# Layer 1 on rows X with W applied behind its loop, attention scalars from raw rows in the last chunk, and a different way to rank the last tile

## The chip, the cores and the metric

The kernel runs on one core of one Trainium2 chip. The core has five engines with their own instruction streams: TensorE (PE in the profile, its weight loads PEld), VectorE (DVE), ScalarE (ACT), GpSimd (POOL) and SyncE (SP, which only issues DMAs here). They meet through semaphores. The metric is the device time of one launch in microseconds; a time below is the median of several executions.

## The reference

There are N = 2708 nodes with D = 128 features, and a dense 2708 x 2708 array `adj` with positive entries where there is an edge. Four layers follow each other, each ending in `x = layernorm(x + layer(x))`.

```python
# layer 0: graph Laplacian with 4 nearest neighbours added
z = leaky_relu(lap(adj, x) @ W1 + b1, 0.1)
S = exp(-sqrt(dist2(z, z) + 1e-10) / 2)        # keep the 4 best of each row
out0 = lap(topk(S) + adj, x) @ W2 + b2         # lap(A, x) = d * (A @ (d * x)), d = rowsum(A) ** -0.5
# layer 1: attention
XW = X @ W
r, c = XW @ a[128:], XW @ a[:128]              # one number a node each
den = exp(leaky_relu(r[:, None] + c[None, :], 0.01))
num = adj @ den
H = adj @ (where(num != 0, den / num, 0) @ XW)
# layers 2 and 3: normalized adjacency, then a linear map; plain adjacency, concat, linear, relu
```

Layer 1 is the costly one: `den` is a full 2708 x 2708 array. Its entry depends only on r of the row, c of the column and the sign of r + c, so for columns sorted by c each row has one cut. The kernel sorts the nodes by c, works on blocks of the sorted order, and forms `adj @ (att @ XW)`. Since `att @ (X @ W)` equals `(att @ X) @ W`, W may stand on either side of that loop.

## The kernel before

Nodes are cut into T = 22 tiles of 128 rows, t = 0 to 21; the last one, t = 21 (`T - 1`, also called `FULL`), has only `LAST` = 20 rows. Columns of `adj` are cut into C = 6 chunks of 512, 512, 512, 512, 384 and 276, which are the tiles 0-3, 4-7, 8-11, 12-15, 16-18 and 19-21. Of the transposed adjacency, the row tiles from 16 on stay in SBUF (`res`); the other 16 are read again in each pass as panels of four tiles (`load_panel`, L178, on SP's queue) into a ring of four slots.

The stages, with their place in the profiled execution:

- Pass 1 of layer 0 and its z (to about 163 us), then the search for the nearest neighbours (to about 305 us): products of z (L647), then DVE's MAX8 and FIND_INDEX8 a tile. Near its end the rows `y2` (scaled input rows) are made and written to DRAM as `y2_rows` by `weigh` (L614, L618). The last write, with tiles 20 and 21, stands on SP's queue; the first panel load of chunk 1 is put behind it with `issue_after`.
- Pass 2 (about 295 to 430 us), `by_panels` with the products at L204. It takes chunk after chunk, 22 products each. After every product `Due.tick` runs the small steps that have come due; `end_pass2` gives each step its tick, counted from the tick n at which its chunk ends. So the code of a step fixes its place in TensorE's, DVE's and ACT's order, which is kept as written (`manual_schedule`). SP and POOL place their own instructions by a scheduler.
- In pass 2, `sum_near` gathers the neighbours' rows of `y2_rows` by indirect DMA on POOL (L677, three a tile) and DVE adds them up (L690); TensorE adds the sum to its accumulator (L697). Then for each chunk: ACT copies the accumulator to hT (L837); `norm0` multiplies by W2 (L725), adds the residual (L730) and normalizes (L276 to L281); `turn` transposes xs (L742) and copies it to xT (L744); `find_c` multiplies xT by the vector `w_c` (L749), which gives c in every row, copies it into `c_row` (L750, the same memory as hT) and takes each row's own c from the diagonal (L754); `times_w` multiplies xT by W, with the two attention vectors as columns 129 and 130 (L762), and copies to `xwe` (L763); `keep_xw` writes the rows to DRAM (L768, POOL).
- The rank of a node by c is counted in the same pass. `compare` makes for tile t a mask of c_row >= c for the columns up to its own (L784, 128 rows; L779 for the last tile, 20 rows by 2708 columns with DVE's own row sum). `rank_rows` sums it along the row on ACT (L797), `rank_columns` sums it down each earlier column block on TensorE (L802, one column of PSUM an earlier tile). `own_ties` (L786) settles equal values in the tile itself.
- After chunk 5, the last one, all this stands alone: its products are done. DVE forms the ranks `rk_f` (L924 to L928), picks out the c at chosen ranks (`pick_c`, L937 to L942, first a coarse `head`, then `first`), TensorE spreads one to all rows (L948), DVE makes `lc` (L977 to L982), finds each node's block (L991 to L1010), and the one-hot arrays (L1018, L1035, L1039). TensorE transposes r onto all rows (L913, `on_all`). Then it begins the block sums (`part_sum`, L1181, about 451 to 508 us), into which `between` puts the rest of the sorting.
- Layer 1's block loop (about 508 to 733 us): for each block of sorted nodes, a gather of adjacency rows (L1306), num (L1428), the reciprocal (L1260 to L1277), and the sum of `att @ XW` with gathered rows of `xw_rows` (L1285, accumulators hacc).
- The result mT is copied (L160 on ACT, L162 on DVE), transposed back to rows by tile (the first ten at L1496, inside the loop; twelve at L1513), scaled (L1498, L1514) and multiplied by `adj`, then layers 2 and 3 by L204 (about 735 to 1066 us).

Of the kernel before, what the change touches and what calls it, by code (L numbers as in the profile page):

```python
# [52 lines left out]
def kernel(  # L53
# [135 lines left out]
    def by_panels(weights, done, tick=None, ready=(), first=None, behind=None):  # L189
# [16 lines left out]
        for c in range(C):  # L206
            w = cw[c]
            for i in [*(first if first and c == 0 else range(FULL)), *([FULL] if c % GROUPS == 0 else [])]:
# [7 lines left out]
                if i < S:  # L216
                    if i % 4 == 0:
                        if ready:
                            part = ready.pop(0)
                        elif behind is not None:  # L220
                            with tc.issue_after(behind):
                                part = load_panel(i // 4, c)
                            behind = None
                        else:
                            part = load_panel(i // 4, c)
                    src = part[:, i % 4, :w]
                else:
                    src = res[:, i - S, cols[c]]
# [138 lines left out]
    xw_rows = dram.tile([N, D], F32, tag="xw_rows", name="xw_rows")  # L367
    with tc.tile_pool(name="knn", bufs=1) as knn:
# [178 lines left out]
        wae = atile([D + 2], "wae")  # L547
        nc.vector.tensor_copy(wae[:, :D], wa_sb)
        for n, half in enumerate((1, 0)):
# [3 lines left out]
                op0=ALU.mult, op1=ALU.mult, accum_out=wae[:, D + n : D + n + 1],  # L553
            )
        w_c = atile([P], "w_c")
        nc.vector.tensor_copy(w_c, wae[:, D + 1 :].to_broadcast([P, P]))
# [33 lines left out]
        def weigh(ts):  # L590
# [22 lines left out]
            queue = nc.gpsimd if t1 < T else nc.sync  # L613
            ins = queue.dma_start(  # L614
                y2_rows[t0 * P : full * P, :].rearrange("(t p) d -> p t d", p=P), y2[:, t0:full, :]
            )
            if full < t1:
                ins = queue.dma_start(y2_rows[FULL * P :, :], y2[:LAST, FULL, :])  # L618
# [3 lines left out]
            return ins.ins  # L622
# [3 lines left out]
        with tc.tile_pool(name="keys", bufs=3) as keys:  # L626
# [28 lines left out]
            written = weigh(range(T - 2, T))  # L655
# [10 lines left out]
    wide = ctx.enter_context(tc.tile_pool(name="wide", bufs=1))  # L666
    xwe = wide.tile([P, T, D + 1], F32, tag="wide", name="xwe")
# [42 lines left out]
    if LAST:  # L710
        nc.gpsimd.memset(xwe[:, FULL, :], 0.0)
        nc.gpsimd.memset(cc[:, FULL:], 0.0)
# [4 lines left out]
    rows_d = atile([T], "rows_d")  # L717
    nc.vector.memset(rows_d, 0.0)
# [3 lines left out]
    def norm0(ts, power=False):  # L722
# [11 lines left out]
        normalize(ts, xs, power)  # L734
# [3 lines left out]
    def turn(c):  # L738
        pt = mis_tile()
        for t in chunk_tiles[c]:  # L740
            o = t * P - starts[c]
            nc.tensor.transpose(pt[:, o : o + pw[t]], xs[: pw[t], t, :], ident[: pw[t], : pw[t]])  # L742
        xTs[c] = sum_pool.tile([P, CW], F32, tag="xT", name="xT", bufs=3)
        nc.scalar.copy(xTs[c][:, : cw[c]], pt[:, : cw[c]])  # L744

    def find_c(c):

        pc = mis_tile()
        nc.tensor.matmul(pc[:, : cw[c]], lhsT=w_c, rhs=xTs[c][:, : cw[c]], start=True, stop=True)  # L749
        nc.scalar.copy(c_row[:, cols[c]], pc[:, : cw[c]])  # L750
        for t in chunk_tiles[c]:
            p, o = pw[t], t * P - starts[c]
            own = small.tile([P, P], F32, tag="junk", name="own")
            nc.vector.scalar_tensor_tensor(  # L754
                own[:p, :p], pc[:p, o : o + p], 1.0, ident[:p, :p], op0=ALU.mult, op1=ALU.mult,
                accum_out=cc[:p, t : t + 1],
            )

    def times_w(c, t):
        p, o = pw[t], t * P - starts[c]  # L760
        po = mis_tile()
        nc.tensor.matmul(po[:p, : D + 1], lhsT=xTs[c][:, o : o + p], rhs=wae[:, : D + 1], start=True, stop=True)  # L762
        nc.scalar.copy(xwe[:p, t, : D + 1], po[:p, : D + 1])  # L763

    def keep_xw(c):
        ts = chunk_tiles[c]
        t0, t1 = ts[0], min(ts[-1] + 1, FULL)
        nc.gpsimd.dma_start(  # L768
            xw_rows[t0 * P : t1 * P, :].rearrange("(t p) d -> p t d", p=P), xwe[:, t0:t1, :D]
        )  # L770
        if t1 <= ts[-1]:
            nc.gpsimd.dma_start(xw_rows[FULL * P :, :], xwe[:LAST, FULL, :D])

    def compare(t):
        p, o = pw[t], t * P
        s = cc[:p, t : t + 1]
        mask = masks[t] = sum_pool.tile([P, N], BF16, tag="mask", name="mask", bufs=3)
        if t in by_dve:
            nc.vector.tensor_scalar(  # L779
                mask[:p, : o + p], c_row[:p, : o + p], s, 0.0, op0=ALU.is_ge, op1=ALU.add,  # L780
                accum_out=rows_m[:p, t : t + 1],
            )
        else:
            nc.vector.tensor_scalar(mask[:p, : o + p], c_row[:p, : o + p], s, None, op0=ALU.is_ge)  # L784
        eq = small.tile([P, P], F32, tag="junk", name="eq")
        nc.vector.scalar_tensor_tensor(  # L786
            eq[:p, :p], c_row[:p, o : o + p], s, not_before[:p, :p], op0=ALU.is_equal, op1=ALU.mult,
# [3 lines left out]
    by_dve = (T - 1,)  # L791

    def rank_rows(t):
        p, w = pw[t], t * P + pw[t]
        if t not in by_dve:
            junk = sum_pool.tile([P, N], BF16, tag="copy", name="junk")
            nc.scalar.activation(junk[:p, :w], masks[t][:p, :w], AF.Copy, accum_out=rows_m[:p, t : t + 1])  # L797

    def rank_columns(t):
        p = pw[t]  # L800
        for u in range(t):
            nc.tensor.matmul(  # L802
                rk[:, u : u + 1], lhsT=masks[t][:p, u * P : (u + 1) * P], rhs=ones_b[:p, :1],
                start=(t == 1 and u == 0), stop=(t == T - 1), skip_group_check=True,
            )


# [5 lines left out]
    def find_r():  # L813
        nc.vector.tensor_copy(rr, xwe[:, :, D])
# [15 lines left out]
    def end_pass2(c, acc):  # L830
# [9 lines left out]
        if c < C - 1:  # L840
            at(n + 2, norm0, ts)
            at(n + 9, turn, c)
            at(n + 11, find_c, c)
            for k, t in enumerate(ts):
                at(n + 13 + 2 * k, compare, t)
                at(n + 14 + 2 * k, times_w, c, t)
                if k == len(ts) - 1:
                    at(n + 14 + 2 * k, keep_xw, c)
                if c == C - 2 and k == len(ts) - 1:
                    behind_last.append(t)  # L850
                else:
                    at(n + 16 + 2 * k, rank_rows, t)
                if t:
                    at(n + 17 + 2 * k, rank_columns, t)
        else:
            for t in behind_last:
                at(n + 1, rank_rows, t)
            at(n + 1, exp_table)
# [765 lines left out]
```

## Time and profile before

| what | value |
|---|---|
| time, median of 3 | 1070.3 us (1069.45 to 1070.99) |
| the profiled execution | 1068.2 us, span 1066.5 us |
| mean granted TensorE clock | 0.976 |
| PE busy | 990.4 us, 93% of the span |
| DVE busy | 643.2 us, 60% |
| ACT busy | 339.1 us, 32% |
| POOL busy | 265.6 us, 25% |
| moved by DMA | 190.30 MB, mean 178 GB/s |

The page of a profile gives busy time, then the span in 40 equal slices, then the chain of work that ended last, then groups of instructions. A line "L204 PE ..." is an instruction written at line 204 of the kernel before. A wait "PE acc L697 <- DVE near_sum L690" says that TensorE stood still before an instruction of L697 until one of L690 had ended on DVE. In the chain each line is a start, a length and the work that the end of the program hangs on.

### The profile page before, as it was taken

To read this page: it belongs to the slowest core of one execution; us is meant where nothing else is said; L and a number is where in the kernel's file an instruction comes from. 1 tells how busy PE (TensorE), PEld (TensorE's weight loads), DVE (VectorE), ACT (ScalarE), POOL (GpSimd) and SP (SyncE) were. 2 spreads that over 40 slices of the span, in tenths; PEclk is the share of its full clock that TensorE was granted. 3 is DMA by queue.
4 is the path that set the end of the run, shared out by engine and by line. 5 is a ranking of instruction groups with operands and counts; after the bars stand their busy time and mean duration, and the time that the engine had idled before them with its cause. 6 is when DMAs were issued, how large, how long until landed. Compare 5 with 4: busy or idle time off the path is not lost.

```text
span 1066.5 us, 11423 instructions
## 1 busy us (share of the span) xinstructions
PE 990.4 (93%) x3678; PEld 479.8 (45%) x3678; DVE 643.2 (60%) x1351; ACT 339.1 (32%) x614; POOL 265.6 (25%) x332
## 2 busy tenths in 40 slices
PE   0898999999998999699899999999999999999996
PEld 0345554444434566444333333334444544564444
DVE  5985438999954678764789999995121111132222
ACT  0000125555510235603767777663010100010000
POOL 4000000000447664107774444440121100000000
PEclk9989999999999999699999999999999999999998
DMA  9999350000056756399655546456765856575652
GB/s 338 367 342 249 115 166 1 0 1 1 22 199 211 239 175 207 126 341 306 165 160 131 147 135 164 137 151 208 226 198 173 291 196 202 159 256 170 225 173 67
DMA packets 109363, 190.30 MB, mean 178 GB/s; under 512 B 13650, under 2 KB 46690, under 8 KB 109294
## 3 DMA queue, kind: packets, MB, share of 16 engines
q1 hardware_dynamic: 91582, 151.86, 43.8%
q0 software_dynamic: 17712, 37.62, 12.7%
q8 instruction: 31, 0.51, 0.2%
q14 instruction: 38, 0.31, 0.1%
HBM read 214.37 MB, written 4.16 MB: 205 GB/s over the span
## 4 chain that ended last, share of the span: by engine, by line
PE 80%; DMA 7%; DVE 6%; issue 2%; POOL 2%; ACT 2%; SPq 1%; POOLq 0%; DVEq 0%; ACTq 0%
PE acc L204 34%; PE acc L647 9%; PE hacc L1285 9%; PE num L1428 9%; PE acc L432 7%; DMA res<-in_adjT 3%; PE acc L637 3%; PE acc L1181 2%; DMA got<-y_rows,where 1%; PE mis L289 1%; DMA part<-in_adjT 1%; DVE mask L784 1%; DVE both L487 1%; POOL ring L125 1%; PE mis L1192 1%
## 5 line engine op out<-in xcount | busy, mean ns | idle before, releaser
L1306 POOL DMA_INDIRECT ring<-in_adjT,slot_i x88 | 98.1, 1115 | 101.0 <-PE num L1428 84.8
L1428 PE MATMUL num<-ring,lw 128*64 128x512 f32 (+1 forms) x528 | 113.6, 551 | 3.6 <-DVE err L1270 1.8
L1285 PE MATMUL hacc<-inv,xws 128*128 128x512 f32 (+1 forms) x264 | 111.7, 559 | 0.5 <-ACT inv L1263 0.3
L647 PE MATMUL acc<-zT,z 128*128 128x512 f32 (+4 forms) x264 | 108.5, 558 | 0.0
L1260 ACT ACTIVATE inv<-num,plain 128x1024 f32<-128x1024 f32 x88 | 80.6, 916 | 59.3 <-PE num L1428 58.1
L257 POOL TENSOR_TENSOR rstd<-rstd,minus_half 128x4 f32<-128x4 f32 (+1 forms) x19 | 18.2, 957 | 313.3 <-DVE rstd L256 313.3
L648 ACT COPY key<-acc 128x512 f32<-128x512 f32 (+3 forms) x132 | 70.2, 535 | 59.7 <-issue 29.8
L238 ACT COPY gb<-acc 128x512 f32<-128x512 f32 (+2 forms) x18 | 9.6, 535 | 249.4 <-PE acc L204 249.4
L204 PE MATMUL acc<-ring,y 128*128 128x512 f32 (+2 forms) x192 | 81.8, 555 | 1.6 <-DMA ring<-in_adjT 1.1
L1270 DVE TENSOR_TENSOR err<-inv,num 128x1024 f32<-128x1024 f32 x88 | 74.4, 853 | 13.3 <-ACT inv L1263 12.5
L1285 PEld LDWEIGHTS hacc<-inv,xws 128*128 128x128 f32 x264 | 46.5, 189 | 77.5 <-issue 37.6
L677 POOL DMA_INDIRECT got<-y_rows,where x66 | 70.1, 1063 | 32.8 <-DMA y_rows<-y 9.3
L1277 DVE SCALAR_TENSOR_TENSOR inv<-gb,g_inv,inv 128x1024 f32<-128x1024 f32 x88 | 77.0, 913 | 0.1
L204 PE MATMUL acc<-ring,xs 128*128 128x512 f32 (+2 forms) x192 | 76.7, 542 | 0.0
L204 PE MATMUL acc<-ring,carry 128*128 128x512 f32 (+2 forms) x192 | 74.5, 542 | 0.0
L204 PE MATMUL acc<-ring,m_rows 128*128 128x512 f32 (+2 forms) x192 | 74.3, 542 | 0.0
L1274 DVE SCALAR_TENSOR_TENSOR inv<-err,inv 128x1024 f32<-128x1024 f32 x88 | 72.6, 863 | 0.1
L647 PEld LDWEIGHTS acc<-zT,z 128*128 128x128 f32 (+1 forms) x264 | 47.6, 188 | 54.9 <-issue 49.5
L1263 ACT ACTIVATE inv<-inv 128x1024 f32<-128x1024 f32 x88 | 67.6, 768 | 2.8
L649 DVE MAX8 near<-key 128x8 f32<-128x2708 f32 (+1 forms) x22 | 65.5, 2978 | 4.8 <-ACT key L648 4.8
L574 POOL TENSOR_TENSOR slot_e<-near,sim 128x44 f32<-128x44 f32 (+2 forms) x3 | 0.7, 244 | 271.5 <-DVE d2inv L602 267.3
L650 DVE FIND_INDEX8 where<-near,key 128x8 uint32<-128x2708 f32 (+1 forms) x22 | 65.4, 2972 | 0.0
(327 smaller groups left out, 1340.0 us busy)
## 6 DMA issues: line engine op xcount, KB each, us to landing
ring<-in_adjT SPq DMA_DIRECT2D x86, 1024.0 KB
ring<-in_adjT SPq DMA_DIRECT2D x19, 768.0 KB
part<-in_adjT SPq DMA_DIRECT2D x12, 1024.0 KB
ring<-in_adjT SPq DMA_DIRECT2D x19, 552.0 KB
res<-in_adjT SPq DMA_DIRECT2D x4, 1280.0 KB
more<-in_adjT SPq DMA_DIRECT2D x4, 1024.0 KB
part<-in_adjT SPq DMA_DIRECT2D x3, 768.0 KB
part<-in_adjT SPq DMA_DIRECT2D x3, 552.0 KB
```

The costliest lines, as they stand in the source:

```text
L204: nc.tensor.matmul(accs[c][: lhsT.shape[-1], :w], lhsT=lhsT, rhs=src, start=start, stop=stop)
L432: nc.tensor.matmul(accs[c][:, : cw[c]], lhsT=y[:, i, :], rhs=src[:, : cw[c]], start=first, stop=last)
L647: nc.tensor.matmul(pks[c][:p, : cw[c]], lhsT=z2[:, :p], rhs=zT[:, cs], start=False, stop=True)
L648: nc.scalar.copy(key[:p, cs], pks[c][:p, : cw[c]])
L677: nc.gpsimd.indirect_dma_start(out=got[:p, :], out_offset=None, in_=y2_rows[:, :], in_offset=bass.IndirectOffsetOnAxis(ap=where[:p, t, k : ...
L1260: nc.scalar.activation(inv, num[:, :w], AF.Ln, scale=plain[:, 0:1], bias=plain[:, 1:2])
L1270: nc.vector.tensor_mul(err, inv, num[:, :w])
L1274: nc.vector.scalar_tensor_tensor(inv, err, 2.0, inv, op0=ALU.subtract, op1=ALU.mult)
L1277: nc.vector.scalar_tensor_tensor(inv, gb[:, col : col + w], g_inv[:, q : q + 1], inv, op0=ALU.max, op1=ALU.mult)
L1285: nc.tensor.matmul(haccs[:, o:e], lhsT=xws[:, q, :], rhs=inv[:, o:e], start=(q == 0), stop=(q == NQ - 1))
L1306: nc.gpsimd.indirect_dma_start(out=rows[i][:KC, n, :], out_offset=None, in_=adj_half[:, :], in_offset=bass.IndirectOffsetOnAxis(ap=slot_i[ ...
L1428: nc.tensor.matmul(num[n * (BJ + 2) : (n + 1) * (BJ + 2), o:e], lhsT=lw[:, 2 * q + n, :], rhs=rows[i][:, n, c0 + o : c0 + e], start=True, ...
```

## The change

It has six parts. Line numbers above are those of the kernel before.

1. W is applied behind layer 1's loop. The loop gathers normalized rows from a DRAM array `x1_rows` in place of `xw_rows`. The transposes of mT become products with W, which gives turned and multiplied rows in one step.
2. r and c no longer come with W. For each tile xT is multiplied by two columns, `w_rc` (`find_rc`); ACT copies r and c to their columns; `turn_c` spreads c along the rows by transposes of the broadcast column. `w_c`, `wae`, `xwe` and `times_w` are gone.
3. In the last chunk the rows are transposed before they are normalized. Mean and deviation are found meanwhile (`last_stats`), and r and c are put right on DVE: (product - mean * sum of w) * deviation's inverse (`last_rc`; the sum, `w_sum`, is found once before the search). The rows themselves are normalized after `pick_c(edge)`.
4. The last tile, of 20 rows, is compared as columns: one comparison 128 x 22 x 20 and 22 small products (`compare_few`). Tile 20's row sum is split between ACT and DVE.
5. The sums down the mask columns come later (tick n + 20, n + 18 in the last but one chunk, in place of n + 17), the row sums one tick later, with five mask buffers in place of three. Small constants (`neg_r`, `fold`, `sel`, the memsets) are made earlier or on POOL.
6. The last write of `y2_rows` stands on POOL's queue, and no panel load is held behind it. The rows of `x1_rows` are written on SP's queue, where `xw_rows` was written on POOL's.

```diff
@@ by_panels
                         if ready:
                             part = ready.pop(0)
-                        elif behind is not None:
-                            with tc.issue_after(behind):
-                                part = load_panel(i // 4, c)
-                            behind = None
@@ weigh
-            queue = nc.gpsimd if t1 < T else nc.sync
-            ins = queue.dma_start(
+            nc.gpsimd.dma_start(
                 y2_rows[t0 * P : full * P, :].rearrange("(t p) d -> p t d", p=P), y2[:, t0:full, :]
             )
             if full < t1:
-                ins = queue.dma_start(y2_rows[FULL * P :, :], y2[:LAST, FULL, :])
+                nc.gpsimd.dma_start(y2_rows[FULL * P :, :], y2[:LAST, FULL, :])
@@ before the search
+        w_sum = atile([2], "w_sum")
+        ps = mis_tile()
+        nc.tensor.matmul(ps[:, :2], lhsT=ones_f, rhs=w_rc, start=True, stop=True)
+        nc.vector.tensor_copy(w_sum, ps[:, :2])
@@ steps of pass 2
+    def rc_of(c, p_of):
+        ts = chunk_tiles[c]
+        po = mis_tile()
+        for k, t in enumerate(ts):
+            p, o = p_of(t), t * P - starts[c]
+            nc.tensor.matmul(po[:p, 2 * k : 2 * k + 2], lhsT=xTs[c][:, o : o + p], rhs=w_rc, start=True, stop=True)
+        return po[:, : 2 * len(ts)].rearrange("p (k v) -> p v k", v=2)
+    def find_rc(c):
+        ts = chunk_tiles[c]
+        both = rc_of(c, lambda t: P)
+        for v, dst in enumerate((rr, cc)):
+            nc.scalar.copy(dst[:, ts[0] : ts[-1] + 1], both[:, v, :])
+    def last_stats():
+        for t in last_ts:
+            st = small.tile([P, 6], F32, tag="st", name="st")
+            nc.vector.bn_stats(st[: pw[t]], xs[: pw[t], t, :])
+            nc.vector.bn_aggr(mv[: pw[t], t, :], st[: pw[t]])
+        inv_sqrt_of(rstd_l, mv[:, l0:l1, 1], LN_EPS, True)
+    def last_rc():
+        both = rc_of(C - 1, lambda t: P)
+        for v, dst in ((1, cc), (0, rr)):
+            nc.vector.scalar_tensor_tensor(
+                dst[:, l0:l1], mv[:, l0:l1, 0], w_sum[:, v : v + 1], both[:, v, :], op0=ALU.mult, op1=ALU.subtract
+            )
+            nc.vector.scalar_tensor_tensor(
+                dst[:, l0:l1], dst[:, l0:l1], -1.0, rstd_l, op0=ALU.mult, op1=ALU.mult
+            )
+    def turn_c(c):
+        pc = mis_tile()
+        for t in chunk_tiles[c]:
+            o = t * P - starts[c]
+            nc.tensor.transpose(pc[:, o : o + P], cc[:, t : t + 1].to_broadcast([P, P]), ident)
         nc.scalar.copy(c_row[:, cols[c]], pc[:, : cw[c]])
-        for t in chunk_tiles[c]:
-            own = small.tile([P, P], F32, tag="junk", name="own")
...
-    def times_w(c, t):
...
-    def keep_xw(c):
+    def keep_x1(c):
...
-        nc.gpsimd.dma_start(
-            xw_rows[t0 * P : t1 * P, :].rearrange("(t p) d -> p t d", p=P), xwe[:, t0:t1, :D]
+        nc.sync.dma_start(
+            x1_rows[t0 * P : t1 * P, :].rearrange("(t p) d -> p t d", p=P), xs[:, t0:t1, :]
         )
+    split = {T - 2: (T - 1) * P // 2}
     def compare(t):
...
-        mask = masks[t] = sum_pool.tile([P, N], BF16, tag="mask", name="mask", bufs=3)
+        mask = masks[t] = sum_pool.tile([P, N], BF16, tag="mask", name="mask", bufs=5)
+        m = split.get(t, o + p)
+        nc.vector.tensor_scalar(mask[:p, :m], c_row[:p, :m], s, None, op0=ALU.is_ge)
+        if m < o + p:
+            nc.vector.tensor_scalar(
+                mask[:p, m : o + p], c_row[:p, m : o + p], s, 0.0, op0=ALU.is_ge, op1=ALU.add, accum_out=rows_h[:p],
+            )
+        own_ties(t)
+    def compare_few():
+        grid = [P, T, LAST]
+        few_m = sum_pool.tile(grid, BF16, tag="few", name="few_m")
+        nc.vector.tensor_tensor(
+            few_m, cc[:, :, None].to_broadcast(grid), c_row[:, None, FULL * P :].to_broadcast(grid), op=ALU.is_ge
+        )
+        for u in range(T):
+            nc.tensor.matmul(
+                rk[:LAST, T - 1 : T], lhsT=few_m[: pw[u], u, :], rhs=ones_b[: pw[u], :1], start=False,
+                stop=(u == T - 1), skip_group_check=True,
+            )
+        nc.vector.tensor_reduce(few_n, few_m, AX.X, ALU.add)
+        own_ties(T - 1)
@@ end_pass2
         if c < C - 1:
             at(n + 2, norm0, ts)
             at(n + 9, turn, c)
-            at(n + 11, find_c, c)
+            at(n + 11, find_rc, c)
+            at(n + 12, keep_x1, c)
+            at(n + 13, turn_c, c)
             for k, t in enumerate(ts):
-                at(n + 13 + 2 * k, compare, t)
-                at(n + 14 + 2 * k, times_w, c, t)
+                at(n + 14 + 2 * k, compare, t)
...
-                    at(n + 16 + 2 * k, rank_rows, t)
+                    at(n + 17 + 2 * k, rank_rows, t)
                 if t:
-                    at(n + 17 + 2 * k, rank_columns, t)
+                    at(n + (20 if c < C - 2 else 18) + 2 * k, rank_columns, t)
         else:
...
             at(n + 2, norm0, ts, True)
-            at(n + 3, turn, c)
-            at(n + 4, find_c, c)
+            at(n + 2, turn, c, True)
+            at(n + 2, exp_table)
+            at(n + 3, last_stats)
+            at(n + 3, last_rc)
+            at(n + 3, turn_c, c)
+            at(n + 3, negate_r)
@@ rank stage
+        on_all(gb, gb_col, 16, T)
         c_part = pick_c(edge, "first")
+        last_norm()
+        keep_x1(C - 1)
@@ layer 1, end (both places)
-                        nc.tensor.transpose(pt[:, (t - t0) * P : (t - t0 + 1) * P], mT[:, t * P : (t + 1) * P], ident)
+                        nc.tensor.matmul(
+                            pt[:, (t - t0) * P : (t - t0 + 1) * P], lhsT=mT[:, t * P : (t + 1) * P], rhs=wa_sb,
+                            start=True, stop=True,
+                        )
...
-            nc.tensor.transpose(pt[:p, :D], mT[:, t * P : t * P + p], ident)
+            nc.tensor.matmul(pt[:p, :D], lhsT=mT[:, t * P : t * P + p], rhs=wa_sb, start=True, stop=True)
```

## The prediction

> **What bounds the kernel now.** I read the slices first, then the windows, then the waits, then the chain. The slices (tenths busy in fortieths of the span, 26.66 us each) show TensorE at 8 or 9 except in slices 12 and 16, where the change acts:
>
> ```profile
> PE   0898999999998999699899999999999999999996
> PEclk9989999999999999699999999999999999999998
> ```
>
> The second is the end of pass 2. In the windows (us; PE, PEld, DVE, ACT, POOL busy; granted clock; DMA share; GB/s) pass 2 is full from 334 to 405, thins, and starves at 430 to 461, with a clock of 0.72; after that DMA is at 0.95:
>
> ```profile
> 334.00:405.00 71.00, 71.00 (x306) 39.68 (x307) 48.20 (x192) 21.91 (x52) 49.99 (x50) 0.98 0.60 184
> 405.00:430.00 25.00, 22.49 (x195) 17.67 (x194) 19.06 (x62) 15.26 (x26) 7.95 (x7) 0.93 0.64 212
> 430.00:461.00 31.00, 19.22 (x157) 11.31 (x156) 24.64 (x73) 13.63 (x23) 4.35 (x4) 0.72 0.47 163
> 461.00:508.00 47.00, 46.12 (x363) 21.74 (x363) 23.19 (x52) 11.22 (x30) 22.16 (x20) 0.96 0.95 316
> ```
>
> Slice 12 is two TensorE waits (us, times, longest):
>
> ```profile
> PE acc L697 <- DVE near_sum L690: 4.0, 1, 4.0
> PE acc L204 <- DMA ring<-in_adjT: 1.1, 1, 1.1
> ```
>
> The chain (start, length, what) says what was late: the first gather, because the last write of the y rows took 6.41 us to land on SP's queue, behind panel loads:
>
> ```profile
> 305.83 0.50 SPq L614
> ...
> 306.38 6.41 DMA y_rows<-y
> ...
> 313.68 0.31 POOL got L677
> ...
> 333.92 0.49 PE acc L697 x2
> ```
>
> At the end of pass 2 the chain leaves TensorE altogether and goes over DVE:
>
> ```profile
> 438.27 1.47 DVE mask L784
> ...
> 441.90 2.96 DVE mask L779 x2
> ...
> 446.45 0.42 DVE head L937
> ...
> 460.64 0.35 PE mis L1248 x2
> ```
>
> Between these stand only DVE's small steps, and 0.73 at 445.02 in which nothing runs.
>
> [...] 0.72 in the starved window, and transposes at L913 0.235 us apart there against 0.145 near 491. [...] 128 columns with only 44 streamed take 0.115 us (L1028).
>
> **Part 1: the y rows go by POOL (start of pass 2).** Removed: SP's two issues and the rule that held the next panel load behind them. Added: two issues on POOL, behind the write at 303.47 (0.88 us). DVE's y is done at 304.46, so they issue at about 304.8 and 306; gathers from POOL land in 2.5 us at least, 2.9 in the middle and 6.2 at most, so I take 4 under load: landed at 310 to 311, first gather 311 instead of 313.68. The gathers follow at 1.30 us each as before, so the sum that TensorE waits for comes **2.7 us** sooner. Bounds: nothing (the last gathers land 5 to 6 us after issue by the chain, and that congestion may remain) to both waits, 3.95 + 1.13 = 5.1.
>
> **Part 2: r and c inside pass 2.** On TensorE a chunk loses the c matmul (2 x 0.43 at L749) and gains 3 or 4 transposes of 0.11 to 0.145 (0.44 to 0.58). Each tile's product with W (129 columns, two passes) becomes one with 2 columns; by the weight load both cost 2 x 0.11: nothing. ACT loses 19 copies of 0.26 us and gains two small ones a chunk (0.2 each); DVE loses 19 own-diagonals of about 0.21. All those were hidden in 334 to 405, where TensorE has no idle time, so they save nothing. What counts is the chain that delays the next chunk: xT, product, two copies on ACT, transposes, copy, mask, instead of xT, product, copy, mask. ACT is in written order, and row sums of up to 2.2 us stand in front of its copies; behind the turned c stand TensorE's panel products. By the new order half a row sum of 1.27 more stands before xT in chunks 2 and 3 (0.64 each), so c of chunk 3 comes 1.3 later than its 405.98. From there to the last copy to hT it was 23.3; the waits and works above, laid out anew, give 22.8: +0.8. I add 0.6, half a row sum, for chunk 4, since the wait of 2.16 us at 415 (L802 for a mask) shows that the chain has no slack there: **+1.4 us**. Bounds: -1 (two ticks of slack and five mask buffers remove half of the 2.16) to +8 (rival D).
>
> The x1 writes move from POOL to SP, seven DMAs in all. Each stands before a ring load. By its order chunk 0's rows are normalized at about 343 and the next ring slot is free at about 344.5; chunks 1 to 4 have similar room: nothing. Without it, panel loads wait and TensorE with them (the 1.1 us wait above is what one such delay cost). POOL loses seven issues of about 0.9 us between gathers, which were not on the chain.
>
> **Part 3: the tail, 429.42 to 460.64.**
> Before, from the copy to hT to the first mask: 438.27 - 429.42 = 8.85. After: product with W2 and residual to 431.65 as before (2.23); last transpose 0.5; copy 0.45; three products of two passes, 0.9 warm or 1.4 at half clock; two of DVE's correction operations 0.4; three transposes 0.85; copy 0.45: 5.8 to 6.3. The mean, variance and POOL's power (0.90) run beside it to about 434.1, when the products are done too. The table load (1.28) lies between ACT's copies and ends before the second. **-2.6**.
> Masks to head, before 446.45 - 438.27 = 8.2. After: mask 19 with its ties 1.73; the split tile 20, 0.81 by the row slope of 0.07 per 128 columns and 1.5 as half of 2.96, ties 0.27; the 128x440 comparison 0.62 (242 elements take 0.41, 484 take 0.66), its reduction 0.5, ties 0.27; seven small rank operations at 0.19, 1.3: 7.0. **-1.2**, the 0.73 idle included.
> The constants between 447.75 and 448.75 move ahead; the head's product then decides: **-0.5**.
> The last chunk's normalization, 3 x 0.28, now stands on DVE before the block search: **+0.85**.
> Sum **-3.4**: the lone-row product comes at 457.2. TensorE's first sums end 458.34 before; they start earlier by the same, so still wait. Bounds: -1 (from 461 DMA is at 0.95, and takes back what loads do not start earlier) to -5.
>
> **Part 4: W at the end of layer 1.** Ten turned blocks at L1496 (1.25 us) become two-pass products; the second pass adds about 0.3 to the path, partly behind hacc. The twelve last ones (0.77 + 0.77 + 0.38) double and stand, in the new order, all before the first L204, paced by DVE's 0.28 each (3.41 for 12): **+1.3** (0.6 to 2). W's sum matmul before the search: **+0.2**.
>
> **Sum.** -2.7 + 1.4 - 3.4 + 1.3 + 0.2 = -3.2. The profiled execution took 1068.2 (span 1066.5 and 1.7 around it), so 1065.0; it lies 2.1 below the median 1070.3, which gives **1067.1**.
>
> **Rivals.**
> B, all gains in full: the y rows land by 309 and both waits go (-5.1), pass 2 keeps its pace (0), tail -3.4, end +1.3, +0.2: -7.0, **1063.3**. For it: the waits exist and one cause feeds both. Against: congestion of the gathers.
> C, nothing: the gathers' landing, 5 to 6 us late in the chain at 319 and 327, decides, not their start: part 1 gives 0.5; the DMA-bound stage keeps half the tail, -1.7; pass 2 +1.4; end +1.5: about -0.3, **1070.3** within 0.2%.
> D, slower: the longer way TensorE, ACT, TensorE in pass 2. TensorE's order is fixed, so a turned c that waits for a copy behind one row sum (1.27 us on average, 2.2 at the end) holds the products behind it; four chunks of 2 us make +8 in place of +1.4, total +3.4: **1074**. For it: 71.00 of 71 busy, so no slack takes up a new wait. Against: two ticks of about 0.9 us lie between the copies and the turn. It decides from 6.7 us of new TensorE waits between 334 and 430.
> The change can also fail to do its work: if SP's other writes now hold the panels, the gain of part 1 is simply passed on; that is in C.
>
> **How the numbers follow.** Forecast 0.45, B 0.17, C 0.21, D 0.17. The range reaches from B's 1063 to 1072.5, part of the way to D; below and above it 0.05 and 0.14 stay out. Two runs cannot be told apart within 0.2% (2.1 us). Of the forecast, whose own range is 1064.5 to 1069.5, four fifths lie below 1068.2: faster 0.17 + 0.36; same 0.09 + 0.18; slower 0.17 + 0.03.
>
> **What the profile after would show.** Part 1: the first gather near 311, the wait at L697 of 1.3 us or less, no ring wait after it. Part 2: TensorE still full to 405; the last copy to hT near 428. Part 3: first tail mask 6 us after that copy, head 7 us later, the lone-row product 28 us after the copy against 31. Part 4: first L204 of layer 2 some 6.3 us after the last hacc begins its last six against 5.0. The forecast is wrong if TensorE waits appear for ACT's copies or a ring load between 334 and 430, if the gathers land no earlier, or if the stage after 461 grows by what the tail saves.

## The result and the profile after

The changed kernel takes 1075.1 us in the median of 20 runs (1068.1 to 1078.2), the kernel before 1068.8 in its 20 (1065.0 to 1073.4). The ratio is 1.0055, with a 95% interval of 1.004 to 1.007: by this ratio 5.9 us slower. The profiled execution took 1076.5 us with a span of 1074.5, against 1068.2 and 1066.5. Its busy times moved little (PE 995.7 us, DVE 638.1).

Cut at fixed points of the program, the two traces compare as follows. Each row is the time from the point of the row above; the last column is what the forecast gave.

| up to | before, us | changed, us | difference | forecast |
|---|---|---|---|---|
| first product of pass 2 | 294.8 | 296.3 | +1.5 | +0.2 |
| last copy to hT (end of pass 2) | 134.5 | 135.8 | +1.3 | -1.3 |
| product of the lone rows | 31.3 | 28.9 | -2.5 | -3.4 |
| first num product of layer 1 | 47.9 | 46.3 | -1.6 | 0 |
| last six hacc products | 221.6 | 222.4 | +0.8 | 0 |
| layer 2's first product on m_rows | 107.3 | 108.9 | +1.6 | +1.3 |
| issue of the last output write | 223.7 | 227.0 | +3.3 | 0 |
| end of the span | 5.3 | 8.9 | +3.6 | 0 |

The tail and W came out near the forecast. The later start of pass 2 turns out below to be chance. Three other rows were not foreseen: pass 2, the last layers, and, where nothing had been expected at all, the few microseconds after the last output write.

The slices of the changed kernel, TensorE busy and its granted clock, in tenths:

```profile
PE   0788999999998998799999999999999999999995
PEclk9989999999999998699999999999999999998998
```

Counted from 0, slice 12 is still 8, slice 16 has risen from 6 to 7, and slice 15 before it has fallen to 8, with a clock of 8 where it was 9. The new dip of the clock near the end (slice 36) lies in layer 3, where nothing was changed: it is one stretch of 6.8 us at half clock from 972.1 on, which loses 3.4 us of full-speed work, about the 3.3 that the table has there. Slices are now 26.86 us, as the span is longer.

The chain of the changed kernel at the start of pass 2 (start, length, what):

```profile
306.22 0.46 POOL y_rows L610
...
306.80 5.15 DMA y_rows<-y
...
312.83 0.32 POOL got L670
...
333.04 0.49 PE acc L690 x2
```

The write of the y rows lands in 5.15 us in place of 6.41, and the first gather comes 16.5 us after the first product of the pass, not 18.8. The waits of TensorE from 290 to 480 (us in total, times, longest):

```profile
PE rk L847 <- DVE mask L824: 5.3, 4, 2.1
PE acc L690 <- DVE near_sum L683: 2.8, 1, 2.8
...
PE mis L732 <- ACT hT L907: 1.5, 1, 1.5
...
PE mis L760 <- ACT xT L753: 0.8, 1, 0.8
```

The wait for the near sums fell from 4.0 to 2.8, and the ring wait of 1.1 is gone. Longer are the waits for ACT in front of W2's product (hT, 1.5 us in place of 0.3) and of the products for r and c (xT, 0.8; before there was none in pass 2). The chain says why:

```profile
419.40 2.00 ACT junk L842 x2
421.40 0.37 ACT xT L753
421.82 1.44 PE mis L760 x6
...
425.31 0.65 PE mis L805 x3
425.99 0.49 ACT hT L806
426.50 1.36 DVE mask L824
427.89 1.62 ACT junk L842
...
430.03 1.15 ACT junk L842
...
432.25 0.28 ACT hT L907
```

A row sum of 2.00 us stands on ACT in front of the copy xT that TensorE waits for, and further row sums stand in front of the last copy to hT. The granted clock is lower too, as the windows show (us; PE, PEld, DVE, ACT, POOL busy; granted clock; DMA share; GB/s), of the changed kernel:

```profile
334.00:405.00 71.00, 70.68 (x315) 39.88 (x313) 45.15 (x166) 20.01 (x46) 48.41 (x46) 0.95 0.62 189
405.00:432.00 27.00, 22.50 (x174) 17.21 (x173) 17.25 (x47) 13.80 (x20) 5.43 (x5) 0.87 0.60 192
```

and of the kernel before in the second stretch:

```profile
405.00:432.00 27.00, 23.29 (x199) 18.07 (x197) 20.19 (x67) 17.24 (x28) 8.44 (x7) 0.94 0.66 214
```

TensorE's clock is 0.95 and 0.87 in place of 0.98 and 0.94: 71 x 0.03 + 27 x 0.07 = 4.0 us of full-speed work less. Its waits grew from 2.5 to 3.9 us in the two stretches, and to 5.4 with the 1.5 us before W2's product, which end at 432.57, behind the second. Clock and waits can't be added up as losses: from chunk 4's copy to the last copy to hT the changed kernel loses 3.4 us to the clock and leaves TensorE idle for 4.7, a variant below (the x rows on GpSimd) loses 5.1 and is idle for 3.2, and both take 22.6 us. What set the length is taken up again below.

The tail, in the chain of the changed kernel:

```profile
439.61 1.55 DVE mask L824
...
441.43 0.83 DVE mask L824
442.26 1.53 DVE mask L826 x2
...
444.07 0.54 DVE few_m L856
444.63 0.61 DVE few_n L864
...
446.30 0.42 DVE head L1001
...
461.01 0.35 PE mis L1301 x2
```

The two halves of tile 20's mask are 0.83 and 1.53, the narrow comparison 0.54 and its sum 0.61. From mask to head it is 6.7 us in place of 8.2.

TensorE at the end of layer 1 in the changed kernel (start, us, what):

```profile
734.00 2.50 PE L1569 MATMUL mis<-w_att,m_rows 128*128 128x128 f32 x20 [1.87 <-ACT m_rows L160]
736.34 1.02 PE L204 MATMUL acc<-ring,carry 128*128 128x512 f32 x2
```

And the end. The closing instructions of the kernel, seen by their source line, have among them DRAINs (durations in ns, smallest, middle and longest; first and last start in us). Before:

```profile
L1620 POOLq DRAIN  x3: 46/102/817, 1061.7 to 1066.2; - x3
```

Changed:

```profile
L1676 POOLq DRAIN  x3: 46/102/7333, 1066.4 to 1074.2; - x3
```

GpSimd's first closing DRAIN takes 7.33 us in place of 0.82. SP is through with its own waits at 1070.2; GpSimd holds the end until 1073.7. That is 3.5 us which no row of the page shows, since a DRAIN is not counted as busy.

### The profile page after: what moved, and what is told of

Read it like the earlier page. It is cut to its first block, busy times and chain, and to the rows that moved or that the text cites. A ratio compares the mean times of both kernels' runs of the same rounds, so it can differ in the third digit from the quotient of the medians.

```text
span 1074.5 us, 11431 instructions
## 1 busy us (share of the span) xinstructions
PE 995.7 (93%) x3713; PEld 485.7 (45%) x3713; DVE 638.1 (59%) x1313; ACT 334.9 (31%) x602; POOL 257.9 (24%) x328
## 4 chain that ended last, share of the span: by engine, by line
PE 79%; DVE 7%; DMA 7%; issue 2%; ACT 2%; POOL 1%; SPq 0%; POOLq 0%; DVEq 0%; ACTq 0%
PE acc L204 33%; PE hacc L1338 9%; PE num L1481 9%; PE acc L642 9%; PE acc L428 7%; PE acc L632 2%; DMA res<-in_adjT 2%; PE acc L1234 2%; DMA got<-y_rows,where 1%; PE mis L285 1%; DVE where L645 1%; DMA ring<-in_adjT,slot_i 1%; DVE both L483 1%; DMA part<-in_adjT 1%; DVE near L644 1%
```

## The experiments

The forecast lacked the DRAIN and undersized pass 2. Two theories on each: that a row belongs to the change, or that it is chance of one execution. Medians and ratios are against the kernel before, run along with each group; a ratio comes from all executions and can differ by up to 0.15% from that of the two medians. In the first group (both kernels again, the y rows, the more columns) the kernel before itself took 1101.3 us. Its trace is 10.3 us longer in pass 2 and 15.8 us longer between the lone rows and the first num product; why is not shown, so the times of this group are compared inside it only.

**Both kernels again.**

> The kernel before once more, unchanged, for its second trace. If the trace of the first is typical: closing DRAIN on GpSimd under 1 us, TensorE's first product of pass 2 at 295 us, no half-clock window between 735 and 1055. If these differ from execution to execution by chance: the start of pass 2 moves by 1 us or more, or a half-clock window of 3.4 or 6.8 us appears in another place.

> The changed kernel once more, unchanged. Of the 8.0 us between the two spans, 1.45 arose before pass 2, 3.4 in the last layer (half-clock window at 972) and 3.5 after the last instruction (GpSimd's closing DRAIN of 7.3 us). Theory chance: these do not come back, span near 1067. Theory change: the DRAIN of about 7 us comes back in every execution (3.5 us of the loss), and pass 2 again has four half-clock windows of 3.4 us in place of two. The first gather again some 16.5 us after the first product of pass 2 against 18.8 before.

The DRAIN came back: 0.82 us before, 7.33 us changed. From the last output write to the end it was 5.4 and 8.7 us. The start of pass 2 (294.7 and 294.3) did not keep its 1.5 us, so that row was chance. The tail kept its gain: 31.3 and 28.1 us. From chunk 4's copy to its row of c it took 11.1 and 18.3 us, 13.0 and 16.4 in the first pair: that too belongs to the change. In layer 3, both executions now had a half-clock stretch, each of 3.4 us.

**The y rows back on SP.**

```diff
-            nc.gpsimd.dma_start(y2_rows[...], y2[:, t0:full, :])
+            queue = nc.gpsimd if t1 < T else nc.sync
+            ins = queue.dma_start(y2_rows[...], y2[:, t0:full, :])
...
+                            with tc.issue_after(behind):
+                                part = load_panel(i // 4, c)
```

> The changed kernel with the last y rows on SP again and the panel load held behind them (part 1 undone). Theory part 1 helps: first gather 18.8 us after the first product again, wait at the near sums 4.0 and a ring wait of 1.1, total 2 to 3 us above the changed kernel, so ratio to before about 1.008. Rival, the gain of part 1 is lost later in pass 2: the same ratio, 1.005 to 1.006. If the closing DRAIN falls below 1 us here, the number of GpSimd DMAs is what lengthens it.

Ratio 1.0037 (1.0015 to 1.006). The first gather came 17.0 us after the first product, 16.5 in the changed kernel of that group. In this group part 1 had hardly anything to gain, so its worth in the total was not settled. The DRAIN is 7.25 us with two DMAs fewer on GpSimd: the y rows do not cause it.

**More columns in the products for r and c.**

```diff
-            nc.tensor.matmul(po[:p, 2 * k : 2 * k + 2], lhsT=xTs[c][:, o : o + p], rhs=w_rc, ...)
+            nc.tensor.matmul(po[:p, 2 * k : 2 * k + D], lhsT=xTs[c][:, o : o + p],
+                             rhs=w_rc[:, None, :].to_broadcast([P, D // 2, 2]), ...)
```

> The changed kernel, but each product for r and c streams 128 columns (the two, repeated) in place of 2, at the same weight loads. Theory clock (two columns leave the array idle, and the half-clock windows in pass 2 come from that): two half-clock windows fewer between 334 and 430, total 2 to 4 us less, ratio to before about 1.002. Rival (waits alone cause them): windows and time as in the changed kernel, 1.005, or up to 0.5 us more.

Ratio 1.0042 (1.0023 to 1.0061), like the kernel above. In the trace the clock from 405 to 445 was 0.91 against 0.83 and 0.85 in the two other changed kernels of the group, but chunk 4 still took 15.9 us from its copy to its row of c, and the last copy to hT came 151.3 us after the first product against 150.7 and 154.1. Inconclusive: the streamed columns may raise the clock, and no time followed.

**The x rows on GpSimd.**

```diff
-        nc.sync.dma_start(x1_rows[t0 * P : t1 * P, :]..., xs[:, t0:t1, :])
+        nc.gpsimd.dma_start(x1_rows[t0 * P : t1 * P, :]..., xs[:, t0:t1, :])
```

> The changed kernel with the x1 rows written on GpSimd's queue, where the XW rows were written before (187 DMAs on GpSimd; before 185, changed 180). Theory A, the XW writes that GpSimd lost make its closing DRAIN 7.3 us long instead of 0.8: the DRAIN is about 0.8 again and the span ends 3.3 to 3.5 us earlier after the last output write than in the changed kernel (5.3 us after its issue in place of 8.8); ratio to before 0.3% lower than the changed kernel's. Rival, the memsets that moved to GpSimd or something else does it: DRAIN stays at 7.3. Rival of the prediction (writes on SP hold panel loads): ring waits of TensorE go away in pass 2; I expect none to be there.

Ratio 1.0029 (1.0013 to 1.0044), in place of 1.0055. The end of this kernel:

```profile
L1676 POOLq DRAIN  x3: 46/102/963, 1064.0 to 1067.4; - x3
```

The span ends 5.2 us after the last output write again. No ring wait of TensorE stands in pass 2 of either: SP's writes held no panel. Theory A holds, and one thing more is to be seen. The last gathers of this kernel on GpSimd are

```profile
708.73 2.12 POOL L1359 DMA_INDIRECT ring<-in_adjT,slot_i  x1 [1.95 <-issue]
711.16 1.05 POOL L1359 DMA_INDIRECT ring<-in_adjT,slot_i  x1 [0.30 <-issue]
712.52 1.63 POOL L1359 DMA_INDIRECT ring<-in_adjT,slot_i  x1 [0.30 <-issue]
```

and of the changed kernel

```profile
710.77 1.04 POOL L1359 DMA_INDIRECT ring<-in_adjT,slot_i  x1 [2.50 <-PE num L1481]
712.12 1.05 POOL L1359 DMA_INDIRECT ring<-in_adjT,slot_i  x1 [0.30 <-issue]
```

Where the DRAIN is short, a gather near the last is long (2.1 us; also in the kernel before, at 714.92), where it is long, none is.

**Pass 2 as before, all else as changed.**

```diff
-            at(n + 11, find_rc, c)
-            at(n + 13, turn_c, c)
+            at(n + 11, find_c, c)      # one product for the row of c, own c from the diagonal
+            at(n + 14, find_r, c)
-                at(n + 14 + 2 * k, compare, t)
+                at(n + 13 + 2 * k, compare, t)
-                    at(n + 17 + 2 * k, rank_rows, t)
+                    at(n + 16 + 2 * k, rank_rows, t)
-                    at(n + (20 if c < C - 2 else 18) + 2 * k, rank_columns, t)
+                    at(n + 17 + 2 * k, rank_columns, t)
```

> The changed kernel, with c in pass 2's first five chunks by one product for the whole row again and the own c from its diagonal, and with masks, row sums and column sums at the ticks of before (part 2 and the later ranks undone, the tail and all else as changed). Theory chain (the longer way and the later ranks cost pass 2 what the gathers gained): from the copy of chunk 4's accumulator to its row of c 13 us in place of 16.4 to 18.9, last copy to hT 3 us earlier relative to the start of pass 2, total 2 to 3 us below the changed kernel. Rival (lost to slow gathers or clock): no difference beyond 0.1%.

Ratio 1.0041 (1.0013 to 1.0069; nine runs). In the trace chunk 4 took 11.8 us from copy to c, and the last copy to hT came 129.5 us after the first product, 6.3 less than in the changed kernel. The window from 405 to 432:

```profile
405.00:432.00 27.00, 21.64 (x197) 16.58 (x197) 19.72 (x67) 17.99 (x24) 5.16 (x4) 0.97 0.72 238
```

The clock is 0.97. The stage answers as the theory of the chain said; the total, 1.0041 against 1.0055 with intervals that overlap, does not confirm the 2 to 3 us.

**Column sums at n + 18.**

```diff
-                    at(n + (20 if c < C - 2 else 18) + 2 * k, rank_columns, t)
+                    at(n + 18 + 2 * k, rank_columns, t)
```

> The changed kernel with the column sums at n + 18 in every chunk in place of n + 20. Theory ranks (the late sums of chunk 3 stand in front of chunk 4's turn on TensorE and wait for masks there): half or more of the loss between chunk 4's copy and its row of c goes, 1 to 1.5 us less in total. Rival (the two copies and the turn of c cost it): no change; or a new wait for masks two ticks earlier, up to 2 us more.

Ratio 1.0083 (1.0057 to 1.0109; six runs), slower than the changed kernel. The waits for masks in pass 2 went to 5.4 us in three, and chunk 4 took 17.8 us. Earlier sums alone make a new wait; with the rest of the order as changed, the late ones are not what costs.

**W left out.**

```diff
-                        nc.tensor.matmul(pt[...], lhsT=mT[:, t * P : (t + 1) * P], rhs=wa_sb, ...)
+                        nc.tensor.transpose(pt[...], mT[:, t * P : (t + 1) * P], ident)
...
-            nc.tensor.matmul(pt[:p, :D], lhsT=mT[:, t * P : t * P + p], rhs=wa_sb, ...)
+            nc.tensor.transpose(pt[:p, :D], mT[:, t * P : t * P + p], ident)
```

> The changed kernel with W left out of layer 1's values (the result is turned without the product, as before the change; attention still uses r and c). Forecast of part 4: 1.3 us less than the changed kernel, between the last sum of the loop and layer 2's second pass. Rival: the second pass of the matmuls is hidden behind DVE's copies, under 0.5 us.

From the last six hacc products to m_rows it took 107.3 us, exactly as before; with W 108.9. So W costs 1.6 us in this stage. Ratio 1.0034 (1.0018 to 1.0051).

**Both losses taken out.** The edits of the x rows on GpSimd and of pass 2 as before, together.

> The changed kernel with both losses taken out: x1 rows written on GpSimd, and pass 2's chain and ranks as before; tail, y rows and W at the end as changed. Theory (closing DRAIN 3.4, part 2 in pass 2 about 4, W at the end 1.7; gathers and tail give 6): DRAIN below 1 us, no half-clock window between 334 and 425, about 4 us below the kernel before, ratio 0.996. Rival (a loss that no stage shows remains): ratio 0.999 to 1.002.

Median 1066.9 against 1069.0, ratio 0.9991 (0.9975 to 1.0007): by the ratios 6.8 us faster than the changed kernel, and not to be told from the kernel before. Against the x rows on GpSimd alone, run in another group, the second edit takes the ratio from 1.0029 to 0.9991, 4.1 us (1.7 to 6.5, estimated from the two intervals). Pass 2's last copy came at 132.9 us. The expected 0.996 was not reached; one reason is in the trace:

```profile
728.15 4.13 PE L1588 MATMUL mis<-w_att,m_rows 128*128 128x128 f32 x20 [1.87 <-ACT m_rows L160]
```

The same twenty W products that took 2.50 us take 4.13 at half clock, and the stage 110.5 us in place of 108.9. Five of the eleven traces with W at the end show 110.5, each with one half-clock stretch of 3.4 us there; none of the five without W goes over 107.3.

**c by product, ticks as changed.**

```diff
-            at(n + 11, find_rc, c)
-            at(n + 13, turn_c, c)
+            at(n + 11, find_c, c)
+            at(n + 14, find_r, c)
```

> The changed kernel with c by one product for the row and the own c from its diagonal at n + 11, r at n + 14, but masks, row sums and column sums at the changed ticks. Theory way (products, copies and turn of c cost pass 2): same gain as with all of part 2 undone, the stretch of 405 to 432 at a clock of 0.94 or more, 3 to 4 us below the changed kernel. Theory ranks (the ticks cost it): clock stays near 0.81 to 0.87 there, time as the changed kernel's within 1 us.

Ratio 1.0043 (1.0027 to 1.0059). Chunk 4 took 13.4 us from copy to c, which is back near 13.0, but the clock from 405 to 432 is 0.87 and the last copy came at 134.9 us. So the way to c makes that part of the chain long. Whether the ticks of before are needed as well is not shown: the ratio is that of all of pass 2 as before (1.0041), and from the first to the last copy to hT the pass took 96.3 us, between the 92.5 of that kernel and the 97.1 with the x rows on GpSimd alone, near the 96.2 of both losses taken out. Neither theory came true as stated.

**Only the last chunk's x rows on GpSimd.**

```diff
+        (nc.gpsimd if c == C - 1 else nc.sync).dma_start(x1_rows[t0 * P : t1 * P, :]..., ...)
```

> The changed kernel with only the last chunk's two x1 writes on GpSimd (182 DMAs; 180 gave a closing DRAIN of 7.3 us, 185 and 187 gave 0.8 to 1.0). If the end depends on how many DMAs GpSimd has issued in all: DRAIN 0.8 to 1 with a longer last gather (1.6 to 2.1 us) where the limit lies below 182, else 7.3 with a last gather of 1.05. I expect 7.3.

DRAIN 7.50 us, and no long last gather.

**The kernel before, a third time.**

> The kernel before once more. The changed kernel and three of its four variants on this kind of chip show a half-clock window of 6.8 us some 29 us into layer 3 (3.4 us lost); the first trace of before shows none, its second one of 3.4 us. Theory phase [...]: it appears here or not, near 29 us after layer 3's first product. Closing DRAIN 0.8.

DRAIN 0.82 us, no half-clock stretch in layer 3; all stages within 0.6 us of the first trace.

**The kernel before with only its XW rows moved to SP.**

```diff
-        nc.gpsimd.dma_start(xw_rows[t0 * P : t1 * P, :]..., xwe[:, t0:t1, :D])
+        nc.sync.dma_start(xw_rows[t0 * P : t1 * P, :]..., xwe[:, t0:t1, :D])
```

> The kernel before with one change alone: its XW rows written on SP's queue in place of GpSimd's (178 DMAs on GpSimd in place of 185). Theory A (GpSimd's lost writes lengthen its closing DRAIN): DRAIN 7.3 us, last gather 1.05 us in place of 2.1, end 3.4 us later after the last output write, ratio 1.003. Rival (the DRAIN needs something else of the change, or the writes on SP hold panels): DRAIN 0.8, or ring waits of TensorE in pass 2. Also open: whether the half-clock window 29 us into layer 3, so far in all eight traces with a long DRAIN and in one of five with a short one, goes with it; chance says no.

Ratio 1.0037 (1.0023 to 1.0051), 4.0 us slower by this edit alone. Its end:

```profile
L1620 POOLq DRAIN  x3: 46/102/7252, 1059.4 to 1067.2; - x3
```

From the last output write to the end it is 8.8 us. This trace, 1.0 us longer than that of before, shows how little one execution says of the total: its pass 2 happened to end 3.9 us sooner after its first product (130.6 us), so that the 3.5 us at the end hardly show in it.

**Seven small writes on GpSimd.**

```diff
+        nc.gpsimd.dma_start(spare[c : c + 1, :], xs[:1, t0, :])
```

> The changed kernel, x1 rows on SP as changed, with seven small writes of one row each added on GpSimd where the chunks' rows are written (187 DMAs on GpSimd, hardly more packets). Theory count (the number of DMAs decides the DRAIN): DRAIN 0.8 to 1 and 3 us less in total, ratio about 1.003. Theory descriptors (what the DMAs carry decides): DRAIN stays at 7.3, ratio about 1.005 to 1.006.

Ratio 1.007 (1.0046 to 1.0094; seven runs), and

```profile
L1679 POOLq DRAIN  x3: 46/102/7497, 1068.5 to 1076.5; - x3
```

With 187 DMAs on GpSimd, as many as with the x rows there, the DRAIN stays. So it is not their number. What they carry separates the cases in all sixteen traces: 17712 and 17776 packets on GpSimd's queue give 0.8 to 1.0 us, 17248 to 17536 give 7.3 to 7.5. Their bytes separate them as well (37.6 and 37.7 MB against 36.2 to 36.5), so packets and bytes are not told apart. This kernel showed no half-clock stretch in layer 3, so that does not go with the DRAIN.

## Why the prediction was wrong

**The step that failed most is one that it did not contain.** Of the x1 writes it said "POOL loses seven issues of about 0.9 us between gathers, which were not on the chain", and costed the move at nothing. It looked for the cost in the queue that the writes joined, SP's, and found none there, rightly. The cost was in the queue that they left: GpSimd's closing DRAIN grew from 0.8 to 7.3 us, 3.6 us at the end of the span. The DRAIN starts at 1066.4 in the changed kernel, and SP's waits for the last output write end only at 1070.2, so only about half of its 7.3 us is seen. The move alone, on the kernel before, costs 4.0 us by the ratio (interval 2.5 to 5.4), and taking it back saves 2.8 of the 5.9 (0.5 to 5.1, estimated from the two intervals). Why a queue that carried less has a longer DRAIN is not shown. Late in the layer 1 loop (from 600 us on) one gather takes 2.1 us in all five traces with a short DRAIN, and in none of the eleven with a long one does a gather there take more than 1.5; whether the two have one cause, no run here shows.

**Part 1.** Right: the first gather came 2.3 us sooner in the pass (forecast 2.7), the first copy to hT 37.3 us after the first product in place of 39.6, and the ring wait went. The wait for the near sums came out at 2.8 us, not at 1.3 or less. Part 1's worth in the total was not isolated.

**Part 2.** Forecast +1.4, measured +3.6: pass 2 ended 1.3 us later though it had gained 2.3 at its start. Cut at chunk 3's row of c, as the forecast did, it has two steps.

Up to that row the forecast was +1.3. From the first copy to hT it took 71.5 us before and 74.2 in the changed kernel, +2.6. But the changed kernel's trace has two half-clock stretches of 3.4 us there and that of before has one. Three more traces of the same order with one such stretch (the x rows on GpSimd, W left out, the last chunk's rows on GpSimd) show 72.5 to 72.7, so +1.1: this step was sized rightly, and about 1.6 of the +3.6 is the chance of one execution.

Behind that row lies the step that failed. From chunk 3's row of c to the last copy to hT the forecast laid out 22.8 us "anew" and added 0.6, half a row sum, for chunk 4: 23.4 in place of 23.3. Measured:

| kernel | us | granted clock there |
|---|---|---|
| before, three traces | 23.3, 23.4, 23.0 | 0.93, 1.00, 1.00 |
| changed | 24.4 | 0.86 |
| changed, five more traces (x rows on GpSimd, W left out, last chunk's rows on GpSimd, seven small writes, y rows on SP) | 24.4 each | 0.79 each |
| changed, second trace | 24.4 | 0.72 |
| before with its XW rows on SP | 22.8 | 1.00 |
| pass 2 as before | 22.6 | 1.00 |
| both losses taken out (the same pass 2) | 24.6 | 0.86 |

So the chain of chunk 4 was undersized by 1.0 us. A whole row sum, 2.00 us, stands before its xT in place of the half one, and the last copy then stands on ACT behind more row sums, while TensorE waits for it (1.5 us). In the changed order it is this chain that sets the length, and not how low the clock falls below 0.86: the length is the same to 0.02 us at 0.86, 0.79 and 0.72. (No trace of this order has the stretch at full clock, so what its first half-clock time costs stays open; the products behind xT took 1.44 us in each.) In the trace with both losses taken out the chain goes over TensorE there, and the same pass 2 takes 2.0 us more at 0.86 than at 1.00. The clocks of the table are means: in the traces of before and of the changed kernel no granted clock is recorded but 0.5 and 1.0, and the half-clock stretches, apart from the one that the end of the span cuts off, are 3.4, 6.8, 17.1 and 20.5 us long.

Undoing part 2 whole took 4.1 us off where the x rows were on GpSimd (1.7 to 6.5), and 1.5 us, not clear of noise, where they were on SP (1.0055 to 1.0041); the steps above explain about 2. Rival D named this place, but priced it at +8 and asked for 6.7 us of new waits; 2.9 came (2.5 to 5.4). That its 1074 lies near the measured 1075.1 is luck, since no DRAIN is in it.

**Part 3.** Right: 31.3 us in every trace with the tail of before, 27.7 to 28.9 in every one with the changed tail; forecast 27.8. Inside it the terms balanced otherwise: from copy to mask 7.5 us in place of the 5.8 to 6.3 (6.3 to 7.0 in the other traces), from mask to head 6.7 in place of 7.0.

**Part 4.** 1.6 us, forecast 1.3. But where a half-clock stretch of 3.4 us falls on the W products it is 3.2 (110.5 in place of 107.3), over the stated bound of 2.

**What stays open.** The four measured terms, with the DRAIN and without rows that were chance, give -2.3 + 3.6 - 2.5 + 1.6 + 3.6 = 4.0 of the 5.9 us; with the tail of the other traces 3.4, and without the chance stretch in pass 2 about 1.8. By the times of many executions the two edits that were undone account for all of it (6.8 us, estimated at 4.4 to 9.1), so the terms read from the traces miss some microseconds. The rest may be half-clock stretches that the change makes more frequent: the mean granted clock over the runs is 0.968 for the changed kernel and 0.974 for before, a part of which is the idle end itself, with 12.6 us at half clock in the changed kernel's trace and 9.5 before. From the first m_rows product to the last write the traces of before show 223.7, 223.7 and 225.4 us, those of changed kernels 223.7 to 227.1, and the length goes with the half-clock stretches in it: none up to 224.0, 3.4 us at 225.4, 6.8 us at 227.0. No run tells whether the change makes them more frequent (6.8 us in seven of the twelve traces of changed kernels, in none of the four others) or whether they fall there by chance. Two readings of the prediction were off apart from that: slice 12 of TensorE is an 8 as slices 1, 3 and 19 are, and rival C's terms add up to +0.7, not to -0.3. The forecast of the time rested on the span being otherwise the same, and one pair of traces cannot show that: single executions of the kernel before lie 8 us apart (1065.0 to 1073.4).

## What to carry to other kernels

When DMAs are moved from one queue to another, look at the queue that they leave as well, and at the end of the program: the closing DRAIN, here 7.3 us in place of 0.8, is not in the busy times, and only the closing instructions by their source line show it. Where an engine order is rearranged around TensorE, find the chain that ends the stage before a low clock is blamed: here one stretch took 24.4 us at 0.86, at 0.79 and at 0.72, because the chain ended on ScalarE. Cut the traces at fixed points of the program for this, not at fixed times. A gain of 0.3% put together from stages is worth little as a forecast as long as a stage may shift by 1.7 us with one half-clock stretch of 3.4 us, as it did here.

## What was not expected of the hardware

GpSimd's closing DRAIN took 0.8 to 1.0 us or 7.3 to 7.5 us and nothing between, in sixteen traces of thirteen kernels, and went with what its queue had carried (at least 17712 packets, or at most 17536). Outside the first group some stages took the same time in every trace except for steps of 1.6 to 1.7 us, and the steps go with the half-clock time recorded in them: from the lone-row product to the first num product 46.3, 47.9, 49.5 or 51.2 us (each within 0.1) with 0, 3.4, 6.8 or 10.2 us at half clock; at the end of layer 1, with W there, 108.9 us without and 110.5 with 3.4. So a half-clock stretch of 3.4 us went with 1.6 to 1.7 us more in these stages; at the end of the changed pass 2, where the chain ends on ScalarE, more of it did not lengthen the 24.4 us.
